# First image of two attention layers on one core: position products ahead of the keys, one projection group per step, value products in step 7, and a bias add with inner runs of 32

## The chip, the cores and the metric

The kernel runs on one core of a Trainium2 chip. The metric is the device time of one execution in microseconds (us): for the kernel before, the median of nine runs, 3508.62 us (3505.91 to 3513.18). Five engines work side by side, each in its own program order: TensorE (PE in the profile; its weight loads are PEld), VectorE (DVE), ScalarE (ACT), GpSimd (POOL) and SyncE (SP), which here only issues DMAs. ScalarE issues some DMAs too; an engine that issues a DMA, or waits to issue it, does nothing else in that time. "SPq" and "ACTq" mark such issues in the trace.

## The reference

Two layers are applied one after the other to x of shape (4, 32, 32, 768) in float32. Each adds to x an attention over the 1024 positions of one image, computed on a group-normalised x (32 groups of 24 channels, over all positions). There are 12 heads of 64 channels. The scores get a bias that depends on the query and on the relative row and column of the key:

```
qkv  = gn(x) @ Wqkv                    # layer 1 adds a bias to it
rel_h = einsum('bhwc,hkc->bhwk', q, Rh)        # 32 numbers per query
rel_w = einsum('bhwc,wkc->bhwk', q, Rw)        # 32 numbers per query
bias = rel_h[..., :, None] + rel_w[..., None, :]   # 32 x 32 = 1024 keys
attn = softmax(scale * q @ k.T + bias)
x    = x + (attn @ v) @ Wproj + bproj
```

Rh and Rw are taken from two small tables by the difference of two coordinates.

## The kernel before

**Units.** There are 8 images in the sense of the program (4 images in each of 2 layers, `im` 0 to 7), 6 pairs of heads in each, so 48 pairs `g`, and for each pair 8 steps `n`, one for each 128 queries. A unit is (pair, step). The channels lie on the partitions; the two heads of a pair are the two halves of the 128 partitions.

**What a pair needs.** `project_in(g, which, i)` makes one half (512 positions) of the pair's queries (`which` 0) or keys (1): 12 matmul calls, each of which the trace shows as two records, then a ScalarE copy and a VectorE add out of PSUM. `project_values(g, i)` makes a quarter of the values of two pairs at once, with two copies and two adds (L259, L260). `positions(g, i)` multiplies half of the queries with the tables (L281), copies the products out with ScalarE into the single buffer of `tmp` (L286) and writes them to scratch in HBM (`tdr`, L288); `diagonals(g)` then reads the relative rows back with 16 DMAs of 32 KB (`rel`, L307), on SP, and for pair 0 half of them on ScalarE's queue. They wait for both halves of `tdr`.

**What a step does.** The loop over the units (from L565) works ahead: in step n of a pair it issues

- `biases` of the unit after the next: one GpSimd add for each head, 128 x 1024 elements, into `sc` (L319, six buffers);
- `scores` of the next unit: 4 matmul calls into two PSUM tiles (L333; there are only these two, so a group of scores waits until VectorE has read the one before it), the row minimum with the bias on VectorE (L342), the exponential with its sum on ScalarE (L346);
- the reads of transposed probabilities that are due (`run(behind)`, L381 in `read_back`);
- `turn(g, n)`: two VectorE transposes of the unit's probabilities into `tb` (L370, three buffers for two heads, each holding two steps), and in odd steps the write of both tiles to scratch (`td`, L373);
- `divide` of the next unit: a VectorE reciprocal (L353) and one GpSimd multiplication for each head (L356);
- filler for TensorE: `take(todo, share)` takes `share` slices from the list of projection groups of the next pair and of output groups. A value of 6 is one group of queries, keys or values;
- in step 6 `weigh(g, (0, 1))`, the product of probabilities and values for the first two quarters of the queries, and in step 2 `weigh(g - 1, (2, 3))` for the other two of the pair before (L399: 32 matmul calls for two quarters).

A quarter is two steps. The four writes of a pair are made in steps 1, 3, 5 and 7. The two lists `behind` and `behind2` change places in each step, so the quarters are read back in step 3, step 4, step 7 and step 0 of the next pair. `pt` has two buffers for each head, so the third read waits until the first quarter's product is done.

**The order is written by hand.** The whole body stands under a manual schedule: each engine runs its instructions in the order of the program. Two lists delay work: what is appended to `later` in one step runs at the head of the step after the next. So the first half of the next pair's queries, made in step 0, is multiplied with the tables in step 2, the second half in step 3, and the 16 diagonal reads stand at the head of step 4 on SP's queue, in front of the read of the second quarter (step 4) and the write of the third (step 5).

**Filler.** `prepare(g)` lists two halves of queries, two of keys and two value groups: 36 slices in all. `put_out` adds output groups, 12 slices a pair, from the fourth pair of the first image on. The shares of the eight steps are `[6, 6, 0, 6, 12, 6, 0, 12]`; for pair 0 `[12, 6, 0, 6, 12, 6, 0, 0]`, where the first 6 belong to pair 0's own values. In pairs 0 to 2 of the first image the 36 slices are used up by the end of step 5, and step 7 has no filler.

**The prologue** (L544 to L563) makes the statistics of the first image, normalises it, then issues both halves of pair 0's queries, the first positions, the first half of the keys, the second positions, the 16 diagonal reads, the second half of the keys, a value group, and the first unit's biases, scores and division. `ps_m`, the PSUM pool of all groups other than scores, has two buffers, so each group waits until the one two before it has been copied out.

Of the kernel before, what the change touches and what calls it, by code (L numbers as in the profile page):

```python
# [36 lines left out]
P = 128  # L37
B, HW, C = 4, 32, 768
# [3 lines left out]
NT = S // P  # L42
# [12 lines left out]
def attention_blocks(ctx: ExitStack, tc: tile.TileContext, a: dict, out: bass.AP):  # L55
# [23 lines left out]
    mid = [dram.tile([C, S], FP, tag=f"mid{b}", name=f"mid{b}") for b in range(B)]  # L79
# [38 lines left out]
    for l in range(LAYERS):  # L118
        tab = const.tile([P, 2, 2 * HW], FP, tag=f"tab{l}", name=f"tab{l}")
        nc.gpsimd.memset(tab, 0.0)  # L120
        for i, ax in enumerate("hw"):
            src = a[f"rel{ax}{l}"]
            n = src.shape[1]
# [23 lines left out]
    def stats(im, c, i, x):  # L147

        if i == 0:
            half_stats[im] = small.tile([P, 2, 6], FP, tag="st", name=f"st_{im}_{c}")  # L150
        st = half_stats[im]
        nc.vector.bn_stats(st[:, i, :], x)  # L152
        if i == 1:
            nc.vector.bn_aggr(mv_of[im][:, c, :], st.rearrange("p i s -> p (i s)"))
# [157 lines left out]
    def biases(g, n):  # L312
        rel = rel_of[g]
        for h in range(2):
            sc = scpool.tile([P, HW, HW], FP, tag="sc", name=f"sc_{g}_{n}_{h}")
            sc_of[g, n, h] = sc

            shape = [P, 4, HW, 8]
            nc.gpsimd.tensor_tensor(  # L319
                sc.rearrange("p (a k) (u l) -> p a (k u) l", a=4, l=8),  # L320
                rel[:, h, 0, n, :].unsqueeze(1).unsqueeze(3).to_broadcast(shape),
                rel[:, h, 1, n, :].rearrange("p (l a) -> p a l", a=4).unsqueeze(2).to_broadcast(shape),
                ALU.add,
            )

# [25 lines left out]
    def divide(g, n):  # L351
        st = st_of[g, n]
        nc.vector.reciprocal(st[:, 2, :], st[:, 1, :])  # L353
        for h in range(2):
            sc = sc_of[g, n, h].rearrange("p k j -> p (k j)")
            nc.gpsimd.tensor_scalar(sc, sc, st[:, 2, h : h + 1], 1.0, ALU.mult, ALU.mult)  # L356
# [70 lines left out]
    def fetch(upto):  # L427

        while fetched[0] <= min(upto, len(parts) - 1):
            im, p, o, i = parts[fetched[0]]  # L430
            c0, c1 = cuts(im)[p : p + 2]
            if i == 0:
                w = wopool.tile([P, NC // 2, P], FP, tag="wo", name=f"wo_{im}_{p}_{o}")
                nc.sync.dma_start(
                    out=w[:, : c1 - c0, :],
                    in_=a[f"wo{images[im][0]}"][o][:, c0 * P : c1 * P].rearrange(
                        "p (c o) -> p c o", o=P
                    ),
                )
                for c in range(c0, c1):  # L440
                    wo_of[im, o, c] = w[:, c - c0, :]
            fetched[0] += 1
        while fetched[1] <= min(upto, len(parts) - 1):
            im, p, o, i = parts[fetched[1]]
            l, b = images[im]
            if (p, o, i) == (0, 0, 0) and im + 1 < NI:
                part_of[im] = dram2.tile([C, S], FP, tag="part", name=f"part_{im}")
            res = iopool.tile([P, HALF], FP, tag="res", name=f"res_{im}_{p}_{o}_{i}")
            res_of[im, p, o, i] = res
            src = srcs[l][b] if p == 0 else part_of[im]  # L450
            nc.sync.dma_start(out=res, in_=src[o * P : (o + 1) * P, i * HALF : (i + 1) * HALF])
            fetched[1] += 1
# [54 lines left out]
    early, mid, later, behind, behind2 = [], [], [], [], []  # L507

    def run(todo):
        while todo:  # L510
            todo.pop(0)()

    def prepare(g):

        todo = [(project_in(g, which, i), NC) for which in range(2) for i in range(2) if g < NPAIR]
        if g % 2:
            return todo + [(project_values(g - 1, i), NC) for i in (2, 3)]
        return todo + [(project_values(g, i), NC) for i in (0, 1) if g < NPAIR]
# [5 lines left out]
    def take(groups, n):  # L524

        while groups and n > 0:
            group, count = groups[0]
            if next(group, None) is None:
                groups.pop(0)
            else:  # L530
                groups[0] = (group, count - 1)
                n -= 1
        while groups and groups[0][1] == 0:
            for _ in groups.pop(0)[0]:
                pass
# [6 lines left out]
    with tc.manual_schedule(engines=ENGINES):  # L542
        for c in range(NC):
            for i in range(2):  # L544
                stats(0, c, i, xn_of[0][c][:, i * HALF : (i + 1) * HALF])
        stages, apply = norm(0)
        for n in sorted(stages):
            stages[n]()
        for c in range(NC):
            apply(c)  # L550
        todo = prepare(0)
        take(todo, 2 * NC)
        mid.pop(0)()
        take(todo, NC)
        mid.pop(0)()
        later.pop()()
        take(todo, 2 * NC)
        run(later)
        fetch(3)
        biases(0, 0)  # L560
        scores(0, 0)
        divide(0, 0)
        biases(0, 1)  # L563

        units = [(g, n) for g in range(NPAIR) for n in range(NT)]  # L565
        for at, (g, n) in enumerate(units):
            im, pair = divmod(g, NP)
            end = im + 1 == NI
            if n == 0:
                shares = [6, 6, 0, 6, 12, 6, 0, 12]  # L570
                ins = (todo if at == 0 else []) + prepare(g + 1)
                if pair < 3:
                    if at == 0:
                        shares = [12, 6, 0, 6, 12, 6, 0, 0]
                    todo = ins + (put_out(im - 1, 1, range(4 * pair, 4 * pair + 4)) if im else [])
                elif pair < NP - 1:
                    todo = ins + put_out(im, 0, range(4 * pair - 12, 4 * pair - 8))
                    if pair == 3 and not end:
                        stages, apply = norm(im + 1)
                else:  # L580
                    todo = ins + put_out(im, 0, range(8, 12))
                    if end:
                        fetch_last()
                        todo += put_out(im, 1, range(12)) + put_out(im, 2, range(0, 12, 2))
                        shares = [6, 6, 0, 6, 6, 2, 0, 4]
            if (pair, n) in loads and not end:
                load_x(im + 1, loads[pair, n])
            if im + 1 < B:
                if (pair, n) in loads0:
                    load_x(im + 1, loads0[pair, n], loads0[pair, n] + AHEAD)  # L590
                if pair < 3 and n in (1, 3, 5, 6):
                    c, i = divmod(4 * pair + n // 2, 2)
                    x = xn_of[im + 1][c % AHEAD][:, i * HALF : (i + 1) * HALF]
                    later.append(lambda c=c, i=i, x=x: stats(im + 1, (c + AHEAD) % NC, i, x))
            run(early)
            early, later = later, early
            if at + 2 < len(units):
                biases(*units[at + 2])
            if at + 1 < len(units):
                scores(*units[at + 1])  # L600
            run(behind)
            behind, behind2 = behind2, behind
            if pair == 3 and n in stages and not end:
                stages[n]()
            if pair == 4 and n in (2, 4, 6) and not end:
                apply(n // 2 - 1)
            share = shares[n]
            first = 3 if n == NT - 1 else 2 if end and pair == NP - 1 and n in (3, 4) else 0
            first = min(first, share)
            take(todo, first)  # L610
            share -= first
            turn(g, n)
            if at + 1 < len(units):
                divide(*units[at + 1])
            if pair == 4 and n == 7 and not end:
                for chunks in ((3, 4), (5,)):
                    take(todo, 3)
                    share -= 3
                    for c in chunks:
                        apply(c)  # L620
            take(todo, share)
            if n == 6:
                weigh(g, (0, 1))
            elif n == 2 and g:
                weigh(g - 1, (2, 3))
        for read in behind:
            read(nc.scalar)
        take(todo, 12)
        for quarter in (2, 3):
            weigh(NPAIR - 1, (quarter,))  # L630
        todo = put_out(NI - 1, 2, range(1, 12, 2))
        take(todo, len(todo))
# [55 lines left out]
```

## Time and profile before

| | us |
|---|---|
| median of nine runs | 3508.62 |
| lowest, highest | 3505.91, 3513.18 |
| profiled execution, its own time | 3513.18 |
| span of its trace | 3511.4 |
| TensorE busy | 3465.8 |
| GpSimd busy, 768 bias adds of it | 2728.5, 1890.7 |
| VectorE busy | 2380.6 |
| first TensorE instruction | 26.89 |
| first bias add, first scores | 58.49, 58.65 |

The profiled execution is the slowest of the nine. Times in the trace count from the start of the span. In a line of groups the columns are: line, engine, operation, output from inputs with shapes, count; then busy time and mean ns of one; then the idle time of the engine before them and what ended it. In a line of the timeline they are: start, duration, engine, line, operation, how many were merged, and in brackets the idle time before them. Lines of the timeline that merge several matmuls run a little into the next one, because matmuls are pipelined; prices are best read from start to start. A line of waits gives the total, the number and the longest.

### The profile page before, as it was taken

To read this page: it belongs to the slowest core of one execution; us is meant where nothing else is said; L and a number is where in the kernel's file an instruction comes from. 1 tells how busy PE (TensorE), PEld (TensorE's weight loads), DVE (VectorE), ACT (ScalarE), POOL (GpSimd) and SP (SyncE) were. 2 spreads that over 40 slices of the span, in tenths; PEclk is the share of its full clock that TensorE was granted. 3 is DMA by queue.
4 is the path that set the end of the run, shared out by engine and by line. 5 is a ranking of instruction groups with operands and counts; after the bars stand their busy time and mean duration, and the time that the engine had idled before them with its cause. 6 is when DMAs were issued, how large, how long until landed. Compare 5 with 4: busy or idle time off the path is not lost.

```text
span 3511.4 us, 55102 instructions
## 1 busy us (share of the span) xinstructions
PE 3465.8 (99%) x21120; PEld 1922.6 (55%) x21120; DVE 2380.6 (68%) x3676; ACT 1226.5 (35%) x2040; POOL 2728.5 (78%) x1546
## 2 busy tenths in 40 slices
PE   6999999999999999999999999999999999999999
PEld 3555555555555555555555555555555555555554
DVE  3666767767677676766667667666676667766666
ACT  2333333343333333333333333333333333333331
POOL 3888877778777787787777887787787787787774
PEclk9999999999999999999999999999999999999999
DMA  3889989899899988998889989899889988898877
GB/s 124 315 298 310 340 301 324 321 315 335 299 321 329 315 310 312 317 316 320 319 302 325 318 295 333 312 329 312 296 324 322 323 299 315 319 323 297 309 277 281
DMA packets 624857, 1084.54 MB, mean 309 GB/s; under 512 B 247120, under 2 KB 310096, under 8 KB 575440
## 3 DMA queue, kind: packets, MB, share of 16 engines
q1 hardware_dynamic: 569008, 1028.29, 83.3%
q10 hardware_dynamic: 55584, 52.72, 4.3%
q8 instruction: 166, 2.72, 0.3%
q14 instruction: 99, 0.81, 0.1%
HBM read 580.59 MB, written 500.27 MB: 308 GB/s over the span
## 4 chain that ended last, share of the span: by engine, by line
PE 96%; DMA 2%; DVE 0%; SPq 0%; issue 0%; ACT 0%; POOL 0%; ACTq 0%; DVEq 0%
PE pj L214 28%; PE s L333 19%; PE av L399 19%; PE o L475 14%; PE pv L249 14%; PE tp L281 3%; DMA tdr<-t 1%; DMA pt<-td 1%; DMA wo<-in_wo 0%; SPq L307 0%; DMA td<-tb 0%; DMA xn<-in_x 0%; DMA per<-mv 0%; DMA rel<-tdr 0%; DVE st L152 0%
## 5 line engine op out<-in xcount | busy, mean ns | idle before, releaser
L319 POOL TENSOR_TENSOR sc<-rel 128x1024 f32<-128x1024 f32 x768 | 1890.7, 2485 | 40.3 <-DMA rel<-tdr 40.3
L356 POOL TENSOR_SCALAR sc<-sc,sm 128x1024 f32<-128x1024 f32 x768 | 852.9, 1124 | 690.6 <-DVE sm L353 684.0
L346 ACT ACTIVATE sc<-sc,sm 128x1024 f32<-128x1024 f32 x768 | 879.3, 1146 | 1372.3 <-DVE sm L342 1370.0
L342 DVE CUSTOM_DVE_ANT_0 sc<-s,sc 128x1024 f32<-128x1024 f32 x768 | 909.6, 1221 | 294.1 <-PE s L333 266.4
L214 PE MATMUL pj<-xn,w 64*128 64x512 f32 x4608 | 1033.2, 591 | 28.9 <-DVE xn L193 26.9
L370 DVE STREAM_TRANSPOSE tb<-sc 128x1024 f32<-128x1024 f32 x768 | 910.8, 1221 | 28.8 <-DMA td<-tb 27.9
L214 PEld LDWEIGHTS pj<-xn,w 64*128 64x128 f32 x4608 | 453.1, 188 | 571.0 <-issue 535.9
L333 PE MATMUL s<-k,q 64*128 64x512 f32 x3072 | 750.9, 599 | 7.0 <-DVE sm L342 6.9
L399 PE MATMUL av<-pt,v 128*64 128x256 f32 x6144 | 689.3, 382 | 4.9 <-DMA pt<-td 4.9
L399 PEld LDWEIGHTS av<-pt,v 128*64 128x64 f32 x6144 | 435.0, 137 | 288.4 <-ACT v L259 35.6
L249 PE MATMUL pv<-wv,xn 64*128 64x256 f32 x4608 | 515.6, 377 | 0.0
L249 PEld LDWEIGHTS pv<-wv,xn 64*128 64x128 f32 x4608 | 448.3, 187 | 91.9 <-issue 30.6
L475 PE MATMUL o<-attn,wo 128*128 128x512 f32 x1080 | 475.8, 597 | 0.2 <-DMA wo<-in_wo 0.2
L333 PEld LDWEIGHTS s<-k,q 64*128 64x128 f32 x3072 | 288.1, 187 | 300.8 <-issue 276.4
L475 PEld LDWEIGHTS o<-attn,wo 128*128 128x128 f32 x1080 | 201.5, 190 | 271.3 <-issue 260.8
L260 DVE TENSOR_TENSOR v<-pv,v 128x256 f32<-128x256 f32 x192 | 81.5, 424 | 274.1 <-ACT v L259 274.1
L259 ACT COPY v<-pv 128x256 f32<-128x256 f32 x192 | 71.4, 372 | 327.9 <-PE pv L249 280.1
L286 ACT COPY t<-tp 128x1024 f32<-128x1024 f32 x96 | 97.2, 1012 | 250.6 <-PE tp L281 152.3
L346 ACT ACTIVATION_READ_ACCUMULATOR sc<-sc,sm 128x1 f32 x768 | 143.2, 186 | 0.0
L230 DVE TENSOR_TENSOR q<-pj,q 128x512 f32<-128x512 f32 x96 | 66.4, 691 | 110.6 <-ACT q L227 59.1
L230 DVE TENSOR_TENSOR k<-pj,k 128x512 f32<-128x512 f32 x96 | 66.3, 691 | 94.4 <-ACT k L227 48.1
L281 PEld LDWEIGHTS tp<-tab,q 64*128 64x128 f32 x1536 | 100.2, 187 | 40.0 <-issue 39.9
(34 smaller groups left out, 786.0 us busy)
## 6 DMA issues: line engine op xcount, KB each, us to landing
td<-tb SPq DMA_DIRECT2D x384, 1024.0 KB, 6.0
pt<-td SPq DMA_DIRECT2D x382, 1024.0 KB, 7.7
tdr<-t ACTq DMA_DIRECT2D x96, 512.0 KB, 6.3
w<-in_wqk SPq DMA_DIRECT2D x96, 384.0 KB, 7.8
rel<-tdr SPq DMA_DIRECT2D x760, 32.0 KB, 2.3
part<-res SPq DMA_DIRECT2D x84, 256.0 KB, 5.4
res<-part SPq DMA_DIRECT2D x84, 256.0 KB, 9.2
wv<-in_wv SPq DMA_DIRECT2D x24, 768.0 KB, 8.8
```

Of the source, the lines that this page charges most:

```text
L214: nc.tensor.matmul(t[:, a, :], lhsT=w[rows, c, :], rhs=xn[c][rows, cols], start=(c == 0), stop=(c == NC - 1),)
L230: nc.vector.tensor_tensor(to, t[1], to, ALU.add)
L249: nc.tensor.matmul(t[:, a, k, :], lhsT=xn[c][rows, (2 * i + k) * P : (2 * i + k + 1) * P], rhs=w[rows, c, :], start=(c == 0), stop=(c == N ...
L281: nc.tensor.matmul(ps[:, h, j, :], lhsT=q[rows, at * P : (at + 1) * P], rhs=tabs[l][rows, :], start=True, stop=True,)
L319: nc.gpsimd.tensor_tensor(sc.rearrange("p (a k) (u l) -> p a (k u) l", a=4, l=8), rel[:, h, 0, n, :].unsqueeze(1).unsqueeze(3).to_broadcas ...
L333: nc.tensor.matmul(ps[h][:, cols], lhsT=q[rows, n * P : (n + 1) * P], rhs=k[rows, cols], start=True, stop=True,)
L342: nc.vector.tensor_tensor_reduce(out=sc, in0=ps[h], in1=sc, scale=-scale, scalar=BIG, op0=ALU.add, op1=ALU.min, accum_out=st[:, 0, h : h + 1],
L346: nc.scalar.activation(sc, sc, AF.Exp, bias=st[:, 0, h : h + 1], scale=-1.0, accum_out=st[:, 1, h : h + 1],)
L356: nc.gpsimd.tensor_scalar(sc, sc, st[:, 2, h : h + 1], 1.0, ALU.mult, ALU.mult)
L370: nc.vector.transpose(tb[:, :, j, :], sc_of[g, n, h])
L399: nc.tensor.matmul(av[rows, at * 2 * P : (at + 1) * 2 * P], lhsT=v_of[g][:, k, rows], rhs=pt_of[g, quarter, h][:, :, k, :], start=(k == 0) ...
L475: nc.tensor.matmul(t, lhsT=wo_of[im, o, c], rhs=attn_of[im * NP + c][:, cols], start=(c == c0), stop=(c == c1 - 1),)
```

## The change

Four things change.

- `biases`: the same 1024 sums for each head, walked in another order. Before, the innermost run is 8 keys of one table row: the first operand is constant, the second steps by 4 elements, the output is contiguous. After, the innermost run has 32: the first operand is contiguous, the second constant, and the output steps by 8 elements.
- Prologue: both position groups of pair 0 stand in front of its keys, and the diagonal reads after the first half of the keys. `later` then holds the weight load first and the diagonals second, hence `pop(1)`.
- Shares in pairs 0 to 2 of the first image: `[6, 6, 0, 6, 6, 6, 6, 0]`, with 12 in step 0 of pair 0. The second half of step 4's work goes to step 5, and that of step 5 to step 6.
- In the same three pairs the value products of the first two quarters move from step 6 to step 7, and `run(behind)` is left out in step 7 and the lists don't change places there, so the third quarter is read back in step 0 of the next pair, ahead of the fourth.

```
-            shape = [P, 4, HW, 8]
+            shape = [P, 4, 8, HW]
             nc.gpsimd.tensor_tensor(
-                sc.rearrange("p (a k) (u l) -> p a (k u) l", a=4, l=8),
-                rel[:, h, 0, n, :].unsqueeze(1).unsqueeze(3).to_broadcast(shape),
-                rel[:, h, 1, n, :].rearrange("p (l a) -> p a l", a=4).unsqueeze(2).to_broadcast(shape),
+                sc.rearrange("p (a k) (u l) -> p a l (k u)", a=4, l=8),
+                rel[:, h, 0, n, :].unsqueeze(1).unsqueeze(2).to_broadcast(shape),
+                rel[:, h, 1, n, :].rearrange("p (l a) -> p a l", a=4).unsqueeze(3).to_broadcast(shape),
                 ALU.add,
             )
...
         take(todo, 2 * NC)
-        mid.pop(0)()
+        run(mid)
         take(todo, NC)
-        mid.pop(0)()
-        later.pop()()
+        later.pop(1)()
         take(todo, 2 * NC)
...
                 if pair < 3:
-                    if at == 0:
-                        shares = [12, 6, 0, 6, 12, 6, 0, 0]
+                    if im == 0:
+                        shares = [6 if g else 12, 6, 0, 6, 6, 6, 6, 0]
...
-            run(behind)
-            behind, behind2 = behind2, behind
+
+            short = im == 0 and pair < 3
+            if n < NT - 1 or not short:
+                run(behind)
+                behind, behind2 = behind2, behind
...
-            if n == 6:
+            if n == 6 + short:
                 weigh(g, (0, 1))
```

## The prediction

> **What bounds the kernel now.** First the page's busy times and the waits of TensorE (PE) by what ended them (columns: us in total, times, longest):
>
> ```profile
> PE 3465.8 (99%) x21120; PEld 1922.6 (55%) x21120; DVE 2380.6 (68%) x3676; ACT 1226.5 (35%) x2040; POOL 2728.5 (78%) x1546
> ```
>
> ```profile
> PE pj L214 <- DVE xn L193: 26.9, 1, 26.9
> PE s L333 <- DVE sm L342: 6.9, 6, 1.7
> PE av L399 <- DMA pt<-td: 4.9, 2, 2.9
> ```
>
> PE bounds the kernel, so only time in which PE idles or runs slowly can be won. The 26.9 us are the input statistics, untouched. The same view from 300 us on has 3 us of waits in all, so nearly everything this edit can win lies before 330 us. Next the stretches of the first image and a later one (length, PE, weight loads, DVE, ACT, POOL busy, PE clock, DMA share, GB/s):
>
> ```profile
> 58.65:120.00 61.35, 57.70 (x338) 36.55 (x334) 38.03 (x62) 25.16 (x43) 53.76 (x30) 0.94 0.57 195
> 120.00:191.00 71.00, 66.64 (x418) 37.54 (x416) 46.19 (x73) 24.91 (x42) 56.47 (x33) 0.95 0.92 320
> 191.00:256.50 65.50, 64.05 (x418) 36.58 (x416) 46.18 (x73) 25.02 (x42) 56.45 (x33) 0.97 0.89 317
> 256.50:320.40 63.90, 62.45 (x420) 36.05 (x418) 45.75 (x78) 27.57 (x45) 56.25 (x33) 1.00 0.94 316
> 800.00:1600.00 800.00, 800.00 (x4908) 444.45 (x4906) 560.11 (x860) 281.99 (x475) 636.14 (x359) 1.00 0.90 317
> ```
>
> The cuts lie at the value products L399 of pairs 0 to 3, so rows two to four are one pair each: equal work, 71, 65.5 and 63.9 us, with the clock below 1 where it is longest. Later PE is full. Now PE's order of time around step 7 of pair 0 (start, duration):
>
> ```profile
> 120.04 4.33 PE L399 MATMUL av<-pt,v 128*64 128x256 f32 x34
> 127.27 5.35 PE L399 MATMUL av<-pt,v 128*64 128x256 f32 x30 [2.90 <-DMA pt<-td]
> 132.55 1.99 PE L333 MATMUL s<-k,q 64*128 64x512 f32 x8
> 135.97 3.43 PE L333 MATMUL s<-k,q 64*128 64x512 f32 x7 [1.43 <-DVE sm L342]
> 138.35 1.06 PE L214 MATMUL pj<-xn,w 64*128 64x512 f32 x1
> 139.21 6.30 PE L214 MATMUL pj<-xn,w 64*128 64x512 f32 x22
> ```
>
> Two score groups meet because step 7 has no filler between; the second waits 1.43 us for PSUM and then runs at about half rate. The 1.43 recurs at 201.50 and 267.01. Last, what VectorE (DVE) does there, the queue SP, and the two GpSimd groups:
>
> ```profile
> 122.92 1.24 DVE L370 STREAM_TRANSPOSE tb<-sc 128x1024 f32<-128x1024 f32 x1
> 129.84 1.25 DVE L370 STREAM_TRANSPOSE tb<-sc 128x1024 f32<-128x1024 f32 x1 [5.67 <-DMA td<-tb]
> ```
>
> ```profile
> 108.97 8.91 SPq L307 DMA_DIRECT2D rel<-tdr  x16
> 117.93 1.00 SPq L381 DMA_DIRECT2D pt<-td  x2
> 119.05 1.12 SPq L373 DMA_DIRECT2D td<-tb  x2
> ```
>
> ```profile
> L319 POOL TENSOR_TENSOR sc<-rel 128x1024 f32<-128x1024 f32 x768 | 1890.7, 2485 | 40.3 <-DMA rel<-tdr 40.3
> L356 POOL TENSOR_SCALAR sc<-sc,sm 128x1024 f32<-128x1024 f32 x768 | 852.9, 1124 | 690.6 <-DVE sm L353 684.0
> ```
>
> DVE stands 5.67 us in step 6 because the td write freeing its buffer sat on SP behind sixteen diagonal reads (8.91 us).
>
> **Room.** PE's warm prices, start to start, from 155 to 183 us: input group 5.15, value group 5.18, scores 1.72, value products 7.06, position group 1.00. A pair without output groups needs 4x5.15 + 2x5.18 + 8x1.72 + 2x7.06 + 2x1.00 = 60.8 us. So the three boundaries lose 71.0-60.8 = 10.2, 65.5-60.8 = 4.7 and 63.8-60.8 = 3.0 us, the first scores another 5.5 (58.65 to 68.01 for 3.9 us of work).
>
> **Prologue: positions first.** No instruction is added; the second position group (16 matmuls, copy, one tdr DMA) moves ahead of the first key group. PE waits 0.52 us there now for q and again for k; only the wait for q stays: -0.5. The second copy (L286) needs the one tmp buffer, so the first tdr write (issued 41.95, about 2.9 as the second took) must land: copy 44.9 to 45.9, tdr to 48.9 instead of 51.72. The diagonals' 16 issues on SP and ACT start 2.8 us earlier; on ACT they now stand behind the first key copy (48.2) and still ahead of the second, whose 7.43 us wait shrinks under PE's value group. First bias 55.7 instead of 58.49. Then DVE binds: its value copies end at 60.0 (60.55-0.5), minimum 61.2 and 62.4, so the second scores start at 61.3 and 62.4 instead of 62.26 and 64.65. PE idles about 2.3 us all the same and restarts slowly; only the later of the two starts moves the end: **-2.2 us** from here on.
>
> **One group per step.** In pairs 0 to 2 the second half of step 4 moves down: value group a to step 5, b to step 6, each with 2 ScalarE copies (0.37), 2 DVE adds (0.42) and, two steps on, its weight DMA. Steps 3 to 6 take 1.72+5.15 = 6.9 us of PE, step 7 1.72+7.06 = 8.8. GpSimd needs 2x2.485+2.21 = 7.2 per step, 57.4 per pair: under 60.8, so PE still leads. Steps 0 to 3 keep their work, and the wait at 100.89 (0.97, tmp again) stays.
>
> **Value products in step 7; third read in the next step 0.** This puts 7.06 us of PE between the two score groups, more than DVE's 1.3, so 1.43 and its slow restart go at all three boundaries. What is late next: value group b's adds are now queued behind the step 6 transposes on DVE. In pair 0 these wait for the td write. Its chain (positions, two tdr, 16 diagonals, pt, td) moves by -2.2 only: 129.84 becomes 127.6, transpose to 128.9, add to 129.5. PE would be through the first six key blocks at 123.6 and idles 5.9 us; the other 40 matmuls take about 6.5 (30 took 5.35 after the 2.9 wait), end 136.0. Before, the scores end at 134.54, and the next 31 matmuls take 10.4 us to 144.93, idling included, for 6.65 warm: that point counts as 134.54 + 3.75 = 138.3. The gain is 2.3 there, of which 2.2 is the prologue's: **-0.1 us**, one stall taking the place of two. Behind these adds on DVE stand the minima of the next scores (2.4 us, through by 133); PE wants their PSUM at 136 and GpSimd's division, then idle, delays only the transposes of step 7, whose write is read much later. In pairs 1 and 2 the td write lands some 29 us after the second position group and the adds about 31, when block 7 wants them at 31.8: no wait, though close. **-4.7 and -3.0**. The two reads moved past turn 7's td issues on SP are wanted 16 us after the products, land (7.7) about 5 us early, and free nothing else.
>
> **DMA.** The pairs held 0.89x65.5 = 58.3 and 0.94x63.8 = 60.0 us of DMA; in 60.8 us that is a share of 0.96 to 0.99. If 0.94 is the most it does, pairs last 62.0 and 63.8: +4.2. If it packs, 0. I take a third, **+1.4**.
>
> **Bias runs.** 768 instructions, same elements; reads become unit step and broadcast, the write steps 32 bytes. No row here has such a write. From below, two passes of L356: 2x1124 = 2248 ns (a single pass, 1124, is the extreme); from above, three in series, 3372. Nearest is the row itself, 2485, whose second read now steps 16 bytes; I take 2.35 us. Up to 2.7 us (16x2.7+17.7 = 60.8) PE covers it in the first image and up to 3.3 later (16x3.3+17.7 = 71, a later pair's 71.7): **0**. The single-pass end would start the second scores little earlier, since DVE binds: under 1 us.
>
> [...] The trace shows only the 2485 beside 2248. [...]
>
> **Sum.** -2.2-0.1-4.7-3.0+1.4 = -8.6 on the profiled execution's 3513.18 (span 3511.4). That is the slowest of nine, 4.56 over the median; from 3508.62 it gives **3500.0**.
>
> **Rivals.**
> - Full gain (0.12): the td write of pair 0 lands before its adds are wanted. For it: the long wait is that of one crowded transfer. Against: SP's order is kept. 10.2 instead of 0.1 and no crowding: -20.1, 3488.5.
> - Swallowed (0.25): DMA crowding or a late td in pairs 1 and 2 brings back a restart. For: 0.9 us of slack in pair 1 and a share of 0.96. Then +4.2 for +1.4 and one 3.0 not won: -2.8, 3505.8. That the moves do nothing, because waits only change names, is its end at 3508.6.
> - Slower (0.13): GpSimd becomes the bound. At 3372 ns a pair is 16x3.372+17.7 = 71.7. Three pairs: 215 for 200.4, +14.6; the 44 later ones (71.7 now) stand at the edge, with up to 0.5 each for unevenness, +22 and the rest: 3545. It decides from about 3.07 us, where 16x3.07+17.7 equals the mean 66.8 of today's pairs. For: the write step. Against: the strided read costs only 237 ns over two passes now.
> - The forecast (0.50) has 3493 to 3507.
>
> **Numbers.** Tails beyond the full gain are small; taking in the bias's upper end gives 3488 to 3545. A measurement here tells about 0.2%, 7 us, from no change. Below 3501.6: the full gain and 0.44 of the forecast, 0.56; within: the rest of it and the swallowed gain, 0.31; above: the slower case, 0.13.
>
> **What will show it.** PE's three 1.43 waits for L342 gone; first bias at 55.7; in pair 0 a PE wait of some 6 us in L399, ended by the DVE value add, and DVE's 5.7 us before L370 kept; L319's mean between 2.25 and 2.7 us; pairs 1 and 2 near 61 to 62 us, and PE's order from pair 3 on merely shifted. I am wrong if L319 exceeds 2.7, or the stall in pair 0 is absent or far longer.

## The result, and the profile after

The change makes the kernel slower: 3519.07 us (median of 9 runs, 3517.74 to 3521.35) against 3508.41 us for the kernel before on the same chips (29 runs). The ratio is 1.0032, with a 95% interval of 1.0024 to 1.0041, so 8 to 14 us. The forecast was 3500.0 and faster.

The profiled execution took 3518.25 us, with a span of 3516.4. The loss arises ahead of 330 us. The value products of pair 3 start at 327.51 instead of 320.37, and the last ones at 3496.67 instead of 3489.75: TensorE's order after pair 3 is only shifted, by 6.9 to 7.1 us. Behind that the changed trace gains 1.9 us back, mostly because its last 30 product records run at full rate (3.67 us for 5.35), so the two spans differ by 5.0. (The traced execution of before took 5 us more than the median of its kind; the last experiment says where.)

TensorE's waits in the changed kernel (us in total, times, longest):

```profile
PE av L399 <- DVE v L260: 8.3, 2, 4.3
PE s L333 <- DVE sm L342: 6.3, 5, 2.2
PE av L399 <- DMA pt<-td: 5.0, 2, 3.2
```

The first line is new: twice the value products wait for VectorE's value adds. The second hardly shrank: the waits of 1.43 us are gone at the boundaries of pairs 0 and 2, but 1.88 us stand at that of pair 1, and the first scores wait 1.44 and 2.24 us instead of 1.72 and 0.73. The stretches of the first image, one pair each, cut at the scores ahead of the value products (length, busy time of PE, weight loads, DVE, ACT, POOL, PE clock, DMA share, GB/s):

```profile
121.90:190.30 68.40, 64.10 (x416) 37.02 (x414) 46.19 (x72) 24.89 (x42) 50.37 (x33) 0.95 0.87 314
190.30:255.70 65.40, 63.52 (x420) 40.08 (x418) 45.90 (x72) 24.78 (x42) 49.20 (x32) 0.97 0.84 303
255.70:325.70 70.00, 62.81 (x411) 35.92 (x408) 41.74 (x71) 25.18 (x41) 43.37 (x28) 0.95 0.86 290
```

The first two hold 60.8 us of work each, the third, a scores group shorter, 59.1. So they lose 7.6, 4.6 and 10.9 us, 23.1 in all, where the kernel before lost 17.9. Another 1.9 us are lost ahead of them, where the same work ends at 121.9 instead of 120.04. Together that is the shift of 7.1. The DMA share is not up but down, 0.84 to 0.87 for 0.89 to 0.94. TensorE's order of time where it waits (start, duration, idle time before):

```profile
123.73 2.81 PE L399 MATMUL av<-pt,v 128*64 128x256 f32 x24
130.84 7.39 PE L399 MATMUL av<-pt,v 128*64 128x256 f32 x40 [4.30 <-DVE v L260]
...
201.12 4.00 PE L333 MATMUL s<-k,q 64*128 64x512 f32 x7 [1.88 <-DVE sm L342]
...
257.50 2.81 PE L399 MATMUL av<-pt,v 128*64 128x256 f32 x24
264.29 7.22 PE L399 MATMUL av<-pt,v 128*64 128x256 f32 x40 [3.98 <-DVE v L260]
...
295.29 3.67 PE L399 MATMUL av<-pt,v 128*64 128x256 f32 x30 [3.21 <-DMA pt<-td]
```

In pairs 0 and 2 the products stop after 24 records, six key blocks, and wait for the add of value group b. The last line is another wait: it makes the other half of pair 2's products last 10.9 us instead of 7.06, and 3.8 of the 10.9 us lost in the third stretch are its own. In pair 1 the value groups of steps 5 and 6 belong to the pairs after it, so its products run through, and it is the next scores that wait. What the waits at the three boundaries have in common is on VectorE:

```profile
129.18 1.25 DVE L370 STREAM_TRANSPOSE tb<-sc 128x1024 f32<-128x1024 f32 x1 [8.23 <-DMA td<-tb]
...
196.60 1.25 DVE L370 STREAM_TRANSPOSE tb<-sc 128x1024 f32<-128x1024 f32 x1 [7.26 <-DMA td<-tb]
...
262.63 1.25 DVE L370 STREAM_TRANSPOSE tb<-sc 128x1024 f32<-128x1024 f32 x1 [7.90 <-DMA td<-tb]
263.80 0.12 DVE L353 RECIPROCAL sm<-sm 128x2 f32<-128x2 f32 x1
263.84 0.40 DVE L260 TENSOR_TENSOR v<-pv,v 128x256 f32<-128x256 f32 x1
```

The second transpose of step 6 waits 7 to 8 us for the third quarter's write, in every pair; before, it waited 5.67 us in pair 0, 0.56 in pair 1 and not at all in pair 2. Behind it stand the reciprocal, the value add and the next scores' minima. SyncE's queue in pair 2 shows why the write is late:

```profile
241.84 7.80 SPq L307 DMA_DIRECT2D rel<-tdr  x16
249.74 0.95 SPq L381 DMA_DIRECT2D pt<-td  x2
250.78 1.31 SPq L373 DMA_DIRECT2D td<-tb  x2
```

The two tiles were transposed by 248.5, but SyncE was still issuing the sixteen diagonal reads and then the second quarter's read (2 MB); the write goes out right behind that read and frees its buffer 11.9 us later. In pair 1 it is the same, with 10.8 us:

```profile
184.75 0.95 SPq L381 DMA_DIRECT2D pt<-td  x2
185.79 1.23 SPq L373 DMA_DIRECT2D td<-tb  x2
```

In pair 1 of the kernel before, where the write was issued 3 us after the read's issue had ended, its buffer was free after 7.8 us:

```profile
183.85 0.96 SPq L381 DMA_DIRECT2D pt<-td  x2
187.90 1.47 SPq L373 DMA_DIRECT2D td<-tb  x2
195.71 1.25 DVE L370 STREAM_TRANSPOSE tb<-sc 128x1024 f32<-128x1024 f32 x1 [0.56 <-DMA td<-tb]
```

The bias add is the part that did what was meant:

```profile
L319 POOL TENSOR_TENSOR sc<-rel 128x1024 f32<-128x1024 f32 x768 | 1547.3, 2084 | 41.2 <-DMA rel<-tdr 37.8 <-DMA res<-in_x 3.5
L356 POOL TENSOR_SCALAR sc<-sc,sm 128x1024 f32<-128x1024 f32 x768 | 853.0, 1122 | 1036.2 <-DVE sm L353 1013.4 <-DMA pt<-td 17.5 <-DMA back<-g 5.3
```

2084 ns for 2485; the 343 us that GpSimd saves turn into its idle time in front of L356 (1036 us for 691).

### The profile page after: what moved, and what is told of

Same layout as the page of the kernel before. It is cut to its first block, busy times and chain, and to the rows that moved or that the text cites. A ratio compares the mean times of both kernels' runs of the same rounds, so it can differ in the third digit from the quotient of the medians.

```text
span 3516.4 us, 55100 instructions
## 1 busy us (share of the span) xinstructions
PE 3462.7 (98%) x21120; PEld 1925.5 (55%) x21120; DVE 2392.1 (68%) x3676; ACT 1226.4 (35%) x2040; POOL 2388.1 (68%) x1546
## 4 chain that ended last, share of the span: by engine, by line
PE 95%; DMA 3%; DVE 1%; issue 0%; SPq 0%; ACT 0%; POOL 0%; DVEq 0%; POOLq 0%; ACTq 0%
PE pj L214 27%; PE s L333 19%; PE av L399 19%; PE o L475 14%; PE pv L249 14%; PE tp L281 3%; DMA td<-tb 1%; DMA pt<-td 1%; DMA xn<-in_x 0%; DVE tb L370 0%; DMA tdr<-t 0%; DVE st L152 0%; DMA wo<-in_wo 0%; DVE sc L342 0%; DMA per<-mv 0%
## 5 line engine op out<-in xcount | busy, mean ns | idle before, releaser
L319 POOL TENSOR_TENSOR sc<-rel 128x1024 f32<-128x1024 f32 x768 | 1547.3, 2084 | 41.2 <-DMA rel<-tdr 37.8
L356 POOL TENSOR_SCALAR sc<-sc,sm 128x1024 f32<-128x1024 f32 x768 | 853.0, 1122 | 1036.2 <-DVE sm L353 1013.4
L342 DVE CUSTOM_DVE_ANT_0 sc<-s,sc 128x1024 f32<-128x1024 f32 x768 | 909.6, 1222 | 299.9 <-PE s L333 267.5
```

The lines of the kernel that those rows point to most:

```text
L319: nc.gpsimd.tensor_tensor(sc.rearrange("p (a k) (u l) -> p a l (k u)", a=4, l=8), rel[:, h, 0, n, :].unsqueeze(1).unsqueeze(2).to_broadcas ...
L342: nc.vector.tensor_tensor_reduce(out=sc, in0=ps[h], in1=sc, scale=-scale, scalar=BIG, op0=ALU.add, op1=ALU.min, accum_out=st[:, 0, h : h + 1],
```

## Experiments

Ratios are against the kernel before, timed beside each version on the same chip, with their 95% intervals.

**The three parts by themselves.** Theory A at this point: the value adds queued behind the step 6 transposes are the loss. Rivals: the bias order (B) or the prologue (C).

The bias order alone: the hunk of `biases` in the diff, on the kernel before.

> The kernel before with the new order of the bias add alone. Theory A (the loss comes from the steps: value adds queued on VectorE behind the step 6 transposes): the bias add falls to about 2084 ns as in the changed kernel, and the time stays within 3 us of before, because GpSimd does not bound TensorE anywhere. Theory B (the shorter adds move the softmax work into a collision with transfers): 4 to 10 us slower.

Measured: 3506.45 us, ratio 0.9991 (0.9982 to 1.0000), mean bias add 2085 ns. It costs nothing and wins at most a little. B falls.

The prologue alone:

```
-        mid.pop(0)()
+        run(mid)
         take(todo, NC)
-        mid.pop(0)()
-        later.pop()()
+        later.pop(1)()
```

> The kernel before with both position groups ahead of the keys and nothing else. Theory A: the diagonals start about 1.5 us earlier, but ScalarE's eight issues last about 7 us instead of 4.4, so the second bias add starts no earlier than before, and the time stays within 3 us; the three boundaries keep their losses of 10.2, 4.7 and 3.0 us. Theory C (the prologue is what costs): 4 us slower or more.

Measured: 3511.36 us, ratio 1.0008 (0.9999 to 1.0017), some 3.5 us with an interval that begins at nothing: short of the 4 us that theory C asked for, so C is neither shown nor excluded here. Its trace, ScalarE's issues and the first bias adds:

```profile
49.67 6.49 ACTq L307 DMA_DIRECT2D rel<-tdr  x8
...
55.33 2.44 POOL L319 TENSOR_TENSOR sc<-rel 128x1024 f32<-128x1024 f32 x1 [37.07 <-DMA rel<-tdr]
60.92 2.41 POOL L319 TENSOR_TENSOR sc<-rel 128x1024 f32<-128x1024 f32 x1 [3.15 <-DMA rel<-tdr]
```

Counted from the first position group (38.75 here, 39.81 and 37.51 in the two traces of before), the diagonals start after 10.9 us instead of 11.9, and the first bias add after 16.6 instead of 18.7 and 17.9. But ScalarE's eight issues last 6.49 us, not 4.43, and the second head's add starts after 22.2 us, where it was 21.1 and 20.3.

The steps alone: the changed kernel with the old bias add and the old prologue.

> The changed kernel with the old bias add and the old prologue: new shares, value products in step 7, third read in the next step 0. Theory A: the waits of the value products for VectorE's value adds are there (about 4 us each in two pairs), the value products of pair 3 start near 327 us instead of 320.4, and the time is 8 to 13 us above before. Theories B and C: less than 4 us above before.

Measured: 3514.84 us, ratio 1.0016 (1.0007 to 1.0025), 7.0 us over before by the medians. The value products of pair 3 start at 326.05. The waits of TensorE:

```profile
PE av L399 <- DVE v L260: 13.2, 2, 6.9
PE av L399 <- DMA pt<-td: 6.7, 3, 2.8
PE s L333 <- DVE sm L342: 4.5, 4, 1.9
```

The 7.0 us lie a little below the 8 to 13 that theory A named, and above what B and C allowed. So most of the loss is the steps', and the medians of the parts add up to 9.1 of 10.7 us (-1.4 + 3.5 + 7.0).

**Are the value adds the cause, or only what stands next in line?** The filler of step 6 is issued ahead of the transposes:

```
             first = 3 if n == NT - 1 else 2 if end and pair == NP - 1 and n in (3, 4) else 0
+            if short and n == 6:
+                first = share
```

> The changed kernel, with one edit: in step 6 of the first three pairs the filler, and so the value group and its adds, is issued ahead of the transposes instead of behind them. Theory A: no wait of the value products for the value adds is left; the value products then wait at most for the read of the second quarter (1 to 3 us), and the time falls 5 to 12 us below the changed kernel, to 3507 to 3514. Rival D (the late write of the third quarter holds TensorE anyway, through the next scores or the reads): less than 3 us below the changed kernel.

Measured: 3517.22 us, ratio 1.0027 (1.0017 to 1.0036): 1.9 us below the changed kernel. The wait for the adds is gone from the trace, but in their place TensorE waits for the minima of the next scores (L342), three times, in the first two with the slow restart:

```profile
135.28 3.53 PE L333 MATMUL s<-k,q 64*128 64x512 f32 x7 [2.12 <-DVE sm L342]
...
203.86 3.83 PE L333 MATMUL s<-k,q 64*128 64x512 f32 x7 [2.25 <-DVE sm L342]
...
268.94 2.69 PE L333 MATMUL s<-k,q 64*128 64x512 f32 x7 [1.18 <-DVE sm L342]
```

Theory A falls as it was put; rival D holds. The transpose that waits blocks VectorE, and whatever TensorE needs next from VectorE is late. The new theory E: the late write of the third quarter is the cause.

**The write taken out of SyncE's queue.** Pairs 0 to 2, third quarter only:

```
+                third = g < 3 and quarter == 2
-                nc.sync.dma_start(out=td, in_=tb.rearrange("p k n i -> p (k n i)"))
+                (nc.scalar if third else nc.sync).dma_start(out=td, in_=tb.rearrange("p k n i -> p (k n i)"))
```

> The changed kernel with the write of the third quarter's probabilities (pairs 0 to 2 only) issued by ScalarE instead of SyncE, so that it no longer stands behind the sixteen diagonal reads and the read of the second quarter. Theory E (all the new waits of TensorE come from that late write, through the second step 6 transpose and whatever VectorE has behind it): in pair 0 the write is issued near 115 us instead of 118.7 and lands near 122 instead of 129.2, in pairs 1 and 2 it lands about 4 to 6 us earlier; VectorE's wait for it falls from 23.4 us over the three pairs to under 10, the value adds and the next minima come in time, and the time falls 8 to 15 us, to 3504 to 3511. Rival F (the transfers themselves are the limit, wherever the write is issued): less than 4 us.

Measured: 3508.27 us, ratio 1.0001 (0.9992 to 1.0010): 10.8 us below the changed kernel. That is the size of its whole loss, and more than the 7.0 us of the steps: the prologue's cost is still in this version, as the runs below say. Rival F falls. The write and the transposes of step 6 in pair 0, then TensorE's waits in the first pairs:

```profile
116.95 0.83 ACTq L374 DMA_DIRECT2D td<-tb  x2
```

```profile
122.31 2.37 DVE L370 STREAM_TRANSPOSE tb<-sc 128x1024 f32<-128x1024 f32 x2
124.60 0.12 DVE L353 RECIPROCAL sm<-sm 128x2 f32<-128x2 f32 x1
124.64 0.40 DVE L260 TENSOR_TENSOR v<-pv,v 128x256 f32<-128x256 f32 x1
```

```profile
130.22 3.67 PE L400 MATMUL av<-pt,v 128*64 128x256 f32 x30 [1.76 <-DMA pt<-td]
192.99 3.67 PE L400 MATMUL av<-pt,v 128*64 128x256 f32 x30 [1.14 <-DMA pt<-td]
255.20 3.67 PE L400 MATMUL av<-pt,v 128*64 128x256 f32 x30 [0.57 <-DMA pt<-td]
281.91 5.35 PE L400 MATMUL av<-pt,v 128*64 128x256 f32 x30 [2.47 <-DMA pt<-td]
```

The write is issued only 1.7 us earlier than in the changed kernel (118.66), but on another queue than the read and 0.2 us ahead of it (117.11), and it frees its buffer within 6.6 us instead of 10.5: both transposes run through, the second near 123.5 instead of 129.18. Pair 1 is alike (write 179.90, read 180.36). In pair 2 the write goes out behind the read, and there the other queue helps little:

```profile
239.56 0.95 SPq L382 DMA_DIRECT2D pt<-td  x2
240.51 1.46 ACTq L374 DMA_DIRECT2D td<-tb  x2
250.11 1.25 DVE L370 STREAM_TRANSPOSE tb<-sc 128x1024 f32<-128x1024 f32 x1 [2.35 <-DMA td<-tb]
```

It frees its buffer after 9.6 us (9.4 to 9.7 at this place in all four versions with the new steps and this write), VectorE waits 2.35, and the adds come just in time. So the early write is shown to be what was missing, but not whether the queue or the place ahead of the read makes it land early: a write on SyncE ahead of the read was not run. No wait of TensorE for VectorE is left at a boundary; what is left are waits of 0.6 to 2.5 us for reads. The pairs from one value product to the next last 63.4, 62.8 and, to pair 3, 65.3 us (starts 124.36, 187.75, 250.53, 315.82).

The same write on ScalarE without the new steps and the new prologue, only with the new bias order:

> The kernel before with the new bias order and the third quarter's write on ScalarE in pairs 0 to 2, without the new steps and without the new prologue. If the new steps earn the three slow restarts that were forecast (7.8 us) once the write is early: 3505 to 3508, that is 3 us or more above the version with the steps. If the steps earn nothing: within 1.5 us of that version.

Measured: 3511.81 us, ratio 1.0011 (1.0002 to 1.0019), above the 3505 to 3508 expected. Without the new steps the early write does not help but hurts (the bias order alone had 0.9991). In its trace the value products of pair 0 wait 4.49 and 1.58 us for the two reads of the second quarter (2.90 in the first trace of before, 1.37 and 2.66 in the second). There they are wanted a step earlier, in step 6, and the write goes out 0.4 us ahead of them; that this is why is argued, not shown. So it is the steps and the early write together that win.

**What the prologue costs.** All 16 diagonal reads of pair 0 on SyncE, in the changed kernel:

```
-                    (nc.scalar if h and not g else nc.sync).dma_start(out=rel_of[g][...], in_=src)
+                    nc.sync.dma_start(out=rel_of[g][...], in_=src)
```

> The changed kernel with all 16 diagonal reads of pair 0 issued by SyncE, none by ScalarE. Theory G (the prologue gains nothing because SyncE goes on to the weight loads while ScalarE's eight issues last 7.0 us, so the second head's rows come late and the second half of the keys is copied out late): the 16 issues end by about 58 us, the weight loads start after them, TensorE's 0.7 us wait for the key add goes, the second bias add starts 1 to 3 us before 62.1, and the time falls 1 to 3 us. Otherwise: no change.

Measured: 3515.64 us, ratio 1.0024 (1.0015 to 1.0033), 3.4 us below the changed kernel by the medians, though the two intervals overlap. The second bias add starts at 58.99 instead of 62.15, and TensorE's wait for the key add is gone.

**The versions with the repairs.** With the write on ScalarE and the old prologue, twice:

> The same with the old prologue (positions on both sides of the first half of the keys). Theory E with a prologue that costs a little (+3.5 us measured by itself, interval about 0 to 6): 2 to 5 us below the run before it, so below the kernel before. If the prologue gives the 2.2 us that were forecast: 2 us above it.

> The best version so far (changed kernel, old prologue, third quarter's write on ScalarE), again on this chip beside the two others: 3500 to 3506, below the kernel before in every comparison; at the three boundaries no wait of TensorE for VectorE, and the stretch from the value products of pair 0 to those of pair 3 near 195 us.

Measured: 3502.96 us, ratio 0.9986 (0.9977 to 0.9995), and 3503.68 us, ratio 0.9991 (0.9982 to 1.0000). The first is 5.3 us below the same version with the new prologue. From the value products of pair 0 to those of pair 3 it took 195.7 us in the first and 193.0 in the second.

With both repairs in the changed kernel:

> The changed kernel with both repairs: the third quarter's write issued by ScalarE in pairs 0 to 2, and all 16 diagonal reads of pair 0 issued by SyncE. Theory G (ScalarE's eight slow issues are what the prologue costs): the two repairs add up, 3 to 5 us below the first repair alone, 3503 to 3506, near the version with the old prologue (3503.0). If the positions ahead of the keys cost in some other way: no less than 3507.

Measured: 3502.66 us, ratio 0.9986 (0.9978 to 0.9995). The repairs add up: 5.6 us below the first alone, by the medians, a little more than expected. Its first bias adds, and the issues ahead of them:

```profile
54.12 2.06 POOL L319 TENSOR_TENSOR sc<-rel 128x1024 f32<-128x1024 f32 x1 [36.92 <-DMA rel<-tdr]
58.04 2.05 POOL L319 TENSOR_TENSOR sc<-rel 128x1024 f32<-128x1024 f32 x1 [1.85 <-DMA rel<-tdr]
```

```profile
48.45 7.73 SPq L307 DMA_DIRECT2D rel<-tdr  x16
56.27 0.88 SPq L106 DMA_DIRECT2D w<-in_wqk  x2
```

The weight loads now start after the diagonals' last issue. Both versions beat the kernel before by 4 to 5 us, 0.09 to 0.14%. That is less than the 0.2% that the prediction set as the least a measurement tells; two of the three intervals lie below 1, the third ends at it.

**The kernel before, once more.**

> The kernel before, once more, for a second trace of it. The profiled execution of before was among the slowest of its runs; expected is the same order with the losses at the first scores and the three boundaries between 15 and 25 us in all, and a span 3 to 8 us shorter, the difference lying ahead of 330 us and in how long TensorE runs slowly after its waits.

Measured: 3507.56 us, span 3505.3, ratio 0.9999 (0.9989 to 1.0010). The value products of pair 0 start at 113.33 instead of 120.04; from there to pair 3 it takes 201.0 us, against 200.3 in the first trace. So the 6.7 us between the two traces lie ahead of that: 1.3 ahead of the first matmul, 1.0 in the first 48, and most of the rest in one restart. In the second trace the first scores restart at full rate, where the first ran at a granted clock of 0.50 from 63 to 69 us:

```profile
59.68 1.12 PE L333 MATMUL s<-k,q 64*128 64x512 f32 x2 [1.44 <-DVE sm L342]
61.57 1.55 PE L333 MATMUL s<-k,q 64*128 64x512 f32 x5 [0.76 <-DVE sm L342]
```

Against this trace the value products of pair 3 in the changed kernel start 13.2 us later (327.51 for 314.36), and the span is 11.1 us longer, close to the difference of the medians, 10.7.

## Why the prediction was wrong

**The step that failed** is the sentence on pairs 1 and 2: the write lands some 29 us after the second position group, the adds follow at 31, "no wait, though close", and with it the terms -4.7 and -3.0. Counted from the end of that group's matmuls, the transposes could go on after 33.8 us in pair 1 (162.8 to 196.6) and 34.5 us in pair 2 (228.2 to 262.6), the adds after 35.0 and 35.7. The 29 come out if the write is priced at 7.8 us, as in pair 1 before, where it had been issued 3 us behind the read of the second quarter. With shorter steps 4 and 5 it is issued right behind that read and takes 10.8 and 11.9 us; its issue also comes 1.6 and 1.2 us later than that reckoning has it. The higher price stood in the prediction's own lines: in pair 0 before, the write went out at 119.05, right behind the read, and freed its buffer at 129.84, after 10.8 us. The prediction named the queue, the buffer and the add, kept 10.8 us for pair 0, and did not see that the change puts pairs 1 and 2 in the same place. It also took pair 1's value group for one that pair 1's products need; there the wait went to the minima (1.88 us).

The later issue begins with the single tmp buffer. ScalarE's second position copy waits for the first tdr write in both pairs and starts 3.0 and 4.0 us after the matmuls, 0.2 in the kernel before; why that write lands late stays open.

```profile
165.77 1.01 ACT L286 COPY t<-tp 128x1024 f32<-128x1024 f32 x1 [7.22 <-DMA tdr<-t]
232.20 1.01 ACT L286 COPY t<-tp 128x1024 f32<-128x1024 f32 x1 [8.57 <-DMA tdr<-t]
```

**The reads moved to step 0: wrong too.** They were to land about 5 us early and free nothing else. SyncE issues four reads together there, and the products of pair 2's other half wait for the last of them, 3.21 us at 295.29.

```profile
272.20 6.01 SPq L381 DMA_DIRECT2D pt<-td  x4
```

A wait for a read, of 1.5 to 5.0 us, stands there in all eight traces with the new steps and in none of the five without them; the early write does not remove it (2.47 us).

**Pair 0, -0.1: right in kind.** A wait for the value add, six key blocks in, was forecast at 123.6, to end at 129.5 and with the products at 136.0; it began at 126.5, ended at 130.8, and the products ended at 138.2. One stall took the place of two. (By the prediction's own prices the sixth block ends at 122.2, 120.04 + 1.72 - 2.2 + 2.65; that changes the length of the wait, not its end.) The chain of the write was to come 2.2 us earlier and came 0.7 earlier, 0.6 of it ahead of the first matmul (26.33 for 26.89).

**Boundaries: the sum came out once the write is early, its parts did not.** In the run with the write on ScalarE the way from the value products of pair 0 to those of pair 3 takes 191.5 us. In the second trace of before it takes 201.0, of which 1.7 us of scores moved in front of the first products. The gain is 7.8 us, and -0.1-4.7-3.0 were forecast for the three boundaries. That the sums agree is luck. The waits of 1.43 us did go, as forecast, but pair by pair the loss over the work was 10.9, 3.0 and 4.7 us and is 2.6, 2.0 and 6.2: gains of 8.3, 1.0 and -1.5 us.

**Prologue, -2.2: wrong in sign.** Two prices in it failed. The first tdr write was to land in 2.9 us and free the tmp buffer; it took 5.2 (issued 41.11, the next copy at 46.31), so the diagonals gained 0.6 to 1.0 us, not 2.8. And ScalarE's eight issues were left at 4.43 us; they lasted 6.5 to 7.0, so the second bias add, which would have started at 58.1 (55.7 + 2.35), started at 62.15, and the second scores waited for it. Alone the prologue costs about 3.5 us by the medians. With the issues moved to SyncE that cost is gone, but a gain over the old prologue isn't shown (3502.66 against 3502.96 and 3503.68). Why the same issues on ScalarE take longer stays open: SyncE's weight loads begin 3 us before the last of them, but holding these back wasn't tried.

**DMA, +1.4: the wrong row.** Crowding was feared as a share of busy time; in the changed kernel the share fell, to 0.84 to 0.87 from 0.89 to 0.94. With the write early, pairs 1 and 2, of which the term speaks, lasted 62.8 and 65.3 us for 60.8 and 59.1 us of work: 8.2 us over, nearly all in waits for reads and the slow records behind them, and above the upper bound of 4.2.

**Bias, 0: right.** 2.35 us was taken, 2.084 measured, and the 0.4 us saved are idle time of GpSimd. It lies below two passes of the one-input row (2248), so no price of the write that steps 32 bytes can be seen in it; reads and write changed together, and their shares aren't separated.

**Rivals and signs.** The one called swallowed named a late write as the thing that would bring a restart back, and gave 3505.8; it came in all three pairs and with the prologue's cost, and went over. The slower rival, GpSimd as the bound, had no part, though the time lies in its range. Of the signs of being wrong that the prediction set, neither came: L319 took 2.084 us, and the stall in pair 0 was there, 4.3 us long. They watched pair 0 and GpSimd, not the write in pairs 1 and 2.

## What to carry to other kernels

When steps get shorter, look at every queue whose issue times don't shrink with them. In pair 0 the third quarter's tiles were transposed by 115.5 instead of 118.0, but SyncE's read went out ahead of their write, which was issued at 118.66 instead of 119.05; VectorE then stood 8.23 us for its buffer, with the value add and the next minima behind that. Moving the work that waits (the adds) won 1.9 us and mostly changed the name of the wait; moving the DMA that everything waits for took back the loss, 10.8 us. And price a transfer by a row that has the same things ahead of it: the same write freed its buffer within 6.6 us when issued ahead of the read, after 7.8 when issued 3 us behind it, after 10.5 to 12.4 when issued right behind it on SyncE's queue, and after 9.4 to 9.7 when issued 0.9 to 1.1 us behind it on ScalarE's.

## What the runs showed of the hardware that was not expected

After nearly equal idle times of 1.4 to 1.7 us TensorE came back at different speeds. In the first trace of before, after 1.72 us, two records took 1.66 us and the granted clock was 0.50 from 63 to 69 us; in the second, after 1.44 us, they took 1.12 us and the next five 1.55, at a granted clock of 1.00. The spread between runs of one kernel goes with this clock. Of 32 timed runs of the kernel before, those with a mean granted clock of 0.997 took 3509.8 to 3513.6 us, with 0.998 3506.3 to 3511.3, with 0.999 3504.5 to 3507.0, and the one with 1.000 3502.9. What decides at which speed TensorE comes back isn't shown.

Eight DMA issues of 32 KB on ScalarE took 4.2 to 4.7 us in seven traces with the old prologue and 6.5 to 7.0 in four with the new one, while the eight beside them on SyncE took 3.8 to 4.3 in both.
